# A four-layer graph network on one core: layer 1 writes its inner sums of adj^T to DRAM, layer 3 loads them as operands

## The chip, the cores and the metric

The kernel runs on one core of a Trainium2 chip. The metric is the device time of one execution in microseconds (us), as the median of several runs. Engines are named as in the profile: PE is the matrix engine (PEld its weight loads), DVE the vector engine, ACT the scalar engine, POOL the GpSimd engine and SP the sync engine. SP and POOL issue the DMAs, each in its own queue.

## What is computed

Four graph layers run one after the other on `x` (2708 rows, 512 features) and one sparse-valued, densely stored matrix `adj` (2708 x 2708, fp32). Each layer normalizes its input, aggregates it over the graph and projects it:

```python
h = relu(layernorm(x))
x = x + relu(dinv * ((adj + I) @ (dinv * h)) @ w0)          # layer 0
h = relu(layernorm(x))
x = x + ((dis * (adj @ (dis * h))) @ W.T + b)               # layer 1
h = relu(layernorm(x))
x = x + relu(dinv * ((adj + I) @ (dinv * h)) @ w2)          # layer 2
h = relu(layernorm(x))
# layer 3: gates from adj @ h, masked softmax of scores over adj
x = x + sigmoid(attn_a * (attn @ (h @ W_sa))
                + attn_b * (adj @ (h @ W_gcnb) + b_gcnb))   # layer 3
```

Layers 0 and 2 use `adj` with a diagonal of ones added, layers 1 and 3 use it plain. All four aggregate over the same matrix.

## The kernel before, in words

**Tiling.** The 2708 nodes are cut into four quarters of 677. Of each quarter 640 rows are five tiles of 128 (`KT` is 5); the 37 left over go into two tail tiles. `adj^T` lies in DRAM as blocks `yb[j, i, u]`: quarter `j` of the rows, quarter `i` of the columns, half `u` of those columns. One block is 128 partitions x 5 x 339 fp32, 847.5 KB. `h` stays on chip, and `agg` holds the transposed result of the aggregation.

**Two levels of a fast product.** `aggregate` (line 665) computes `h^T adj^T` with a seven-product scheme in place of eight, at two levels. The outer level splits `h` into XA, XB, XC, XD and `adj^T` into a 2 x 2 of big blocks; `OUTER` (line 426) lists the seven outer products 1 to 7, each with its left operand and the name of its right one. The right operand is a part of `adj^T` (`y11`, `y21`, `y22`) or a sum of such parts (`t1` to `t4`), which layer 0 has computed and kept in DRAM as `osum`. The order of a layer is 1, 7, 2, 4, then the tails of two quarters, 6, 5, then the tails of the other two, then the projection of the first half of the tiles (`epilogue(H1)`), then 3, then `epilogue(H2)`.

Each outer product (`outer_product`, line 516) runs twice, for u = 0 and u = 1. Call one such run a stage. A stage loads the four blocks o11, o12, o21, o22 of its right operand (`load_o`, line 438, issued from SP). Then `inner_y` (line 500) adds on DVE the inner sums of the same scheme: t1 = o12 + o11 (line 509), t2 = o22 + t1 (line 510), t4 = o21 + t2 (line 511), and t3 = o22 + o12, written over o12 (line 513). If the right operand carries a diagonal that has to go, or lacks one, `add_loops` (line 454) first corrects o11 and o22. The operands are numbered 1 (o11), 2 (o21), 3 (o22), 4 (t4), 5 (t1), 6 (t2), 7 (t3). `multiply` (line 544) runs the seven inner products in the order 1, 6, 2, 7, 5, 4, 3, each over five row tiles (`product`, line 535), and puts their sums together on DVE and ACT.

**Buffers.** Blocks live in seven places of `obuf`; the list `free` hands them out in turn, and a stage gives its four back at its end. The sums t1, t2, t4 take slots of `tpool`, which has three under one tag. A slot or a place is used again when all that reads it is done.

**Order of the work.** The program is written in order of layers; the framework's scheduler then sets one fixed order of instructions for every engine and queue, with waits between them, and instructions on one engine need not keep the order of the text. In layer 3 other work lies between the products: dot products of `h` with score vectors (`h_dots`, line 997), row scales (line 1074), and reloads of `h` (`again`, line 1062). Layers 1 and 3 both call `aggregate` with `self_loops` false (lines 961 and 1188), so their inner sums are the same numbers. After layer 3's aggregation follows the attention part, from line 1189 on, which doesn't use the inner sums.

**On POOL's queue** in layer 1 are the loads of `x` tiles (`load_x`, line 911) and the stores of the new ones (line 932), both in `next_x`.

Of the kernel before, what the change touches and what calls it, by code (L numbers as in the profile page):

```python
# [8 lines left out]
FP = mybir.dt.float32  # L9
# [3 lines left out]
P = 128  # L13
# [5 lines left out]
KT = Q // P  # L19
R0 = 32  # L20
R1 = Q - KT * P - R0
U = 2
W = (Q + 1) // U
# [14 lines left out]
def gnn_kernel(  # L38
# [20 lines left out]
    nc = tc.nc  # L59
# [3 lines left out]
    tpool = ctx.enter_context(tc.tile_pool(name="tpool", bufs=3))  # L63
# [4 lines left out]
    dram = ctx.enter_context(tc.tile_pool(name="dram", bufs=1, space=bass.MemoryType.DRAM))  # L68
# [12 lines left out]
    for k in range(1, P // G):  # L81
# [10 lines left out]
    dinv = const.tile([P, NT], FP, name="dinv")  # L92
    dis = const.tile([P, NT], FP, name="dis")
# [7 lines left out]
    xs = [dram.tile([P, D], FP, name=f"xs{t}") for t in range(NT)]  # L101
# [5 lines left out]
        for a in range(2)  # L107
        for b in range(2)
        for u in range(U)
    }  # L110

    h = big.tile([P, NT, D], FP, name="h")
# [14 lines left out]
    free = list(in_obuf)  # L127
# [285 lines left out]
    def other_roots():  # L413
# [12 lines left out]
    OUTER = {  # L426
        1: (XA, "y11", 1),
        2: (XC, "y21", 0),
        3: (XC, "y22", 1),
        4: (XD, "t4", 2),  # L430
        5: (XB, "t1", 1),
        6: (XA, "t2", 2),
        7: (XA, "t3", 1),
    }
    PLAIN = {"y11": (0, 0), "y12": (0, 2), "y21": (2, 0), "y22": (2, 2)}
    QUAD = [(0, 0), (0, 1), (1, 0), (1, 1)]

    def load_o(key, a, b, u):
        blk = free.pop(0)
        if key in PLAIN:  # L440
            j, i = PLAIN[key]
            nc.sync.dma_start(blk, yb[j + a, i + b, u])
        else:
            nc.sync.dma_start(blk, osum[key, a, b, u])
        return blk
# [8 lines left out]
    def add_loops(blk, u, times):  # L454

        for k in range(KT):
            lo, hi = max(k * P, u * W), min((k + 1) * P, (u + 1) * W)
            if lo < hi:
                o = blk[:, k, lo - u * W : hi - u * W]
                nc.vector.scalar_tensor_tensor(  # L460
                    o, ident[:, lo - k * P : hi - k * P], float(times), o, ALU.mult, ALU.add
                )

    def by_halves(f, *xs):

        for ts in (slice(0, KT), slice(KT, 2 * KT)):
            f(*(x[:, ts] for x in xs))

    def minus_sum(o, a, b):
        nc.vector.scalar_tensor_tensor(o, a, -1.0, b, ALU.mult, ALU.subtract)  # L470
# [12 lines left out]
    def inner_x(X, s3=None):  # L483
        n = half // 2
        x11, x12 = X[:, 0:n, 0:P], X[:, n : 2 * n, 0:P]
        x21, x22 = X[:, 0:n, P : 2 * P], X[:, n : 2 * n, P : 2 * P]
        s1, s2, s4 = (
            spool.tile([P, U * W], FP, tag=f"s{k}", name=f"s{k}")[:, 0 : KT * P].rearrange(
                "p (k f) -> p k f", k=KT
            )  # L490
            for k in (1, 2, 4)
        )
        if s3 is None:
            s3 = inner_x3(X)
        minus_sum(s2, x22, s3)
        nc.vector.tensor_sub(s1, x21, x22)
        nc.vector.tensor_add(s4, x12, s2)
        return {1: x11, 2: x12, 3: s4, 4: x22, 5: s1, 6: s2, 7: s3}

    def inner_y(blks, u, loops, t3=None, t3_first=False):  # L500
        o11, o12, o21, o22 = blks
        if loops:
            add_loops(o11, u, loops)
            add_loops(o22, u, loops)
        t1, t2, t4 = (tpool.tile([P, KT, W], FP, tag="t", name=f"t{k}") for k in (1, 2, 4))
        t3 = o12 if t3 is None else t3
        if t3_first:
            nc.vector.tensor_add(t3, o22, o12)
        nc.vector.tensor_add(t1, o12, o11)
        nc.vector.tensor_add(t2, o22, t1)  # L510
        at_y.append(nc.vector.tensor_add(t4, o21, t2).ins)  # L511
        if not t3_first:
            at_y[-1] = nc.vector.tensor_add(t3, o22, o12).ins
        return {1: o11, 2: o21, 3: o22, 4: t4, 5: t1, 6: t2, 7: t3}

    def outer_product(p, self_loops, *dests, at=None):

        X, key, times = OUTER[p]
        with tc.issue_after(at) if at is not None else nullcontext():
            xs_ = inner_x(X)  # L520
        if key in PLAIN:
            loops = times if self_loops else 0
        else:
            loops = 0 if self_loops else -times
        for u in range(U):
            blks = [load_o(key, a, b, u) for a, b in QUAD]
            with tc.issue_after(at) if at is not None else nullcontext():
                ys = inner_y(blks, u, loops)
            multiply(xs_, ys, u, dests)
            free.extend(blks)  # L530

# [100 lines left out]
    def tails(self_loops, qs, loaded=None):  # L632


        at = at_pe[-1]
        for n, q in enumerate(qs):
            blk, pieces = loaded[n] if loaded else tail_rows(self_loops, q)
            for u in range(U):
                tl = pieces[u]
                ps = [  # L640
                    (ps_agg if c < NC - 1 else ps_out).tile(
                        [P, W], FP, tag="agg" if c < NC - 1 else "out", name="pt"
                    )
                    for c in range(NC)
                ]
                with tc.issue_after(at) if loaded else nullcontext():
                    tail_products(ps, tl, True)
                for c in range(NC):
                    d = agg[:, c // 2, q // 2, c % 2, q % 2, u * W : (u + 1) * W]
                    at_end.append(nc.vector.tensor_add(d, d, ps[c]).ins)  # L650
            if blk is not None:
                free.append(blk)
# [5 lines left out]
    def first_part_of_both():  # L658
        nc.scalar.copy(agg[:, 0, 1], agg[:, 0, 0])
# [2 lines left out]
        nc.vector.tensor_add(agg[:, 1, 1], agg[:, 1, 1], agg[:, 0, 1])  # L662
        nc.vector.tensor_add(agg[:, 1, 0], agg[:, 1, 0], agg[:, 1, 1])

    def aggregate(self_loops, epilogue, hooks=None):


        def outer(p, *dests):
            outer_product(p, self_loops, *dests)
            if hooks is not None and p in hooks:  # L670
                hooks[p]()

        outer(1, (0, 0, "as it is"))
        first_part_of_both()
        by_halves(nc.vector.tensor_sub, XA, XA, XB)
        outer(7, (1, 1, "as it is"))
        nc.vector.tensor_sub(XB, XB, XD)
        outer(2, (0, 0, "added"))
        minus_sum(XA, XD, XA)
        nc.vector.tensor_add(XC, XC, XA)  # L680
        outer(4, (1, 0, "as it is"))
        tails(self_loops, (0, 1))
        outer(6, (0, 1, "added"))
        ends_of_sums()
        outer(5, (0, 1, "less"), (1, 1, "less"))
        tails(self_loops, (2, 3))
        epilogue(H1)
        outer(3, (0, 1, "added"))
        epilogue(H2)
# [221 lines left out]
    def load_x(t, src):  # L911
        xt = take(xt_places)
        nc.gpsimd.dma_start(xt, src[t])
        return xt

    def next_x(ts, w_sb, scale, bias, src, colscale, after=None):
        for g in groups(ts):
            n, t0 = len(g), g[0]
            mv = small.tile([P, KT, 2], FP, tag="mv", name="mv")
            xts = []  # L920
            for s, t in enumerate(g):
                xt = load_x(t, src)
                po = project(w_sb, t)
                y = new_y()
                if bias is None:
                    nc.scalar.activation(y, po, AF.Relu, scale=scale[:, t : t + 1])
                else:
                    nc.vector.scalar_tensor_tensor(
                        y, po, scale[:, t : t + 1], bias, ALU.mult, ALU.add
                    )  # L930
                nc.vector.tensor_add(xt, xt, y)  # L931
                nc.gpsimd.dma_start(xs[t], xt)  # L932
                stats(xt, mv[:, s, :])
                xts.append(xt)
            rstd = rstd_of(mv, n)
            if colscale is not None:
                nc.vector.tensor_mul(rstd[:, :n], rstd[:, :n], colscale[:, t0 : t0 + n])
            sh = shift_of(mv, rstd, n)
            for s, t in enumerate(g):
                normalized(t, xts[s], rstd[:, s : s + 1], sh[:, s : s + 1])  # L940
                if after is not None:
                    after(t)
# [15 lines left out]
    w1_sb = load_w(w1)  # L958
    b1_bc = misc[:, 0:D]
    nc.gpsimd.dma_start(b1_bc, b1.partition_broadcast(P))  # L960
    aggregate(False, lambda ts: next_x(ts, w1_sb, dis, b1_bc, xs, dinv))


    def broadcast_columns(po, cs):
# [105 lines left out]
    hooks = {p: lambda ts=ts: h_dots(ts) for p, ts in parts.items()}  # L1070
# [85 lines left out]
    sums = misc[:, 0 : 2 * U * W + NQ * (R0 + R1)]  # L1156
# [28 lines left out]

    hooks[6] = row_scales
    hooks[3] = lambda: again(range(half, NF), slice(0, D // 2))
    aggregate(False, gated_and_ready, hooks)
    wsa_sb = load_w(wsa)
    todo = []  # L1190
    for n, (q, u, b) in enumerate(steps):
# [35 lines left out]
        elif todo:  # L1227
            t, se_t = todo.pop(0)
# [70 lines left out]
```

## Time and profile before

| what | value |
|---|---|
| median of 3 runs | 2097.07 us (2093.76 to 2097.89) |
| profiled execution | 2098.61 us |
| its span in the profile | 2096.7 us |
| granted PE clock, mean | 0.997 |
| layer 1, from its first product to its last projection | about 452 to 833 us |
| layer 3, aggregation and first part of the gates | about 1215 to 1620 us |
| moved by DMA | 360.86 MB |
| HBM read, written | 294.61 MB, 62.15 MB |

The profile is of one execution. Busy time is summed for each engine; the idle time just before an instruction is given together with what ended it. "DMA share" is the mean busy share of the core's 16 DMA engines. A line such as L510 is a line of the kernel before, as printed above. An instruction in the profile that reads `t<-obuf,t` writes the buffer family `t` and reads `obuf` and `t`. SPq and POOLq are the DMA queues of SP and POOL.

### The profile page before, as it was taken

To read this page: it belongs to the slowest core of one execution; us is meant where nothing else is said; L and a number is where in the kernel's file an instruction comes from. 1 tells how busy PE (TensorE), PEld (TensorE's weight loads), DVE (VectorE), ACT (ScalarE), POOL (GpSimd) and SP (SyncE) were. 2 spreads that over 40 slices of the span, in tenths; PEclk is the share of its full clock that TensorE was granted. 3 is DMA by queue.
4 is the path that set the end of the run, shared out by engine and by line. 5 is a ranking of instruction groups with operands and counts; after the bars stand their busy time and mean duration, and the time that the engine had idled before them with its cause. 6 is when DMAs were issued, how large, how long until landed. Compare 5 with 4: busy or idle time off the path is not lost.

```text
span 2096.7 us, 20100 instructions
## 1 busy us (share of the span) xinstructions
PE 2054.8 (98%) x7340; PEld 1279.6 (61%) x7340; DVE 1416.4 (68%) x2481; ACT 409.2 (20%) x833; POOL 182.8 (9%) x330
## 2 busy tenths in 40 slices
PE   5999999999999999999999999999999999999998
PEld 2566655656666554666665556666777666666665
DVE  4578877657767777766686889867538755666512
ACT  1430001130000011100002120000117533444411
POOL 0110111120000012000002120000001000000011
PEclk9999999999999999999999999999999999999999
DMA  9998594555545354654445574555451223233220
GB/s 368 302 373 260 188 342 171 188 190 170 175 154 186 126 189 136 242 174 161 166 145 175 195 244 164 169 166 183 153 176 59 101 99 117 81 103 102 90 74 26
DMA packets 79746, 360.86 MB, mean 172 GB/s; under 512 B 10668, under 2 KB 15660, under 8 KB 79520
## 3 DMA queue, kind: packets, MB, share of 16 engines
q1 hardware_dynamic: 50672, 245.43, 34.0%
q0 software_dynamic: 28976, 114.15, 16.8%
q8 instruction: 58, 0.95, 0.2%
q14 instruction: 40, 0.33, 0.0%
HBM read 294.61 MB, written 62.15 MB: 170 GB/s over the span
## 4 chain that ended last, share of the span: by engine, by line
PE 87%; DVE 6%; DMA 4%; issue 1%; ACT 1%; POOL 0%; SPq 0%; POOLq 0%; DVEq 0%; ACTq 0%
PE pe L1202 17%; PE po L200 15%; PE pc L538 14%; PE pd L538 14%; PE pa L538 13%; PE pb L538 7%; PE pt L600 3%; DMA obuf<-in_yb_dram 2%; DMA ends<-in_yt_dram 1%; PE pt L605 1%; PE pe L600 1%; DVE ends L1001 1%; DMA ends<-xs 1%; PE dg_ps L321 1%; DVE t L511 0%
## 5 line engine op out<-in xcount | busy, mean ns | idle before, releaser
L1202 PE MATMUL pe<-obuf,h 128*128 128x339 f32 x1280 | 373.2, 448 | 0.0
L200 PE MATMUL po<-ends,agg 128*128 128x512 f32 (+2 forms) x968 | 352.1, 521 | 1.3 <-DVE ends L1058 1.0
L538 PE MATMUL pa<-obuf,h 128*128 128x339 f32 x1040 | 317.1, 449 | 2.5 <-ACT h L252 1.4
L1202 PEld LDWEIGHTS pe<-obuf,h 128*128 128x128 f32 x1280 | 240.8, 189 | 127.1 <-issue 10.8
L200 PEld LDWEIGHTS po<-ends,agg 128*128 128x128 f32 x968 | 181.3, 190 | 154.3 <-issue 137.4
L538 PEld LDWEIGHTS pa<-obuf,h 128*128 128x128 f32 x1040 | 195.6, 190 | 110.0 <-issue 9.8
L1119 ACT ACTIVATE e<-r,nsr 128x339 f32<-128x339 f32 x352 | 170.9, 565 | 25.0 <-DVE obuf L1123 11.5
L538 PE MATMUL pb<-t,s 128*128 128x339 f32 x560 | 171.2, 452 | 1.8 <-DVE s L470 1.0
L538 PE MATMUL pc<-t,h 128*128 128x339 f32 x560 | 169.5, 448 | 2.1 <-DVE u L585 2.1
L538 PE MATMUL pd<-t,s 128*128 128x339 f32 x560 | 169.0, 448 | 0.0
L538 PE MATMUL pd<-obuf,s 128*128 128x339 f32 x550 | 166.5, 448 | 1.3 <-DVE s L554 0.9
L572 ACT COPY v<-pa 128x339 f32<-128x339 f32 x56 | 24.6, 439 | 724.7 <-PE pa L538 698.8
L538 PEld LDWEIGHTS pb<-t,s 128*128 128x128 f32 x560 | 106.2, 190 | 57.2 <-DVE t L510 2.1
L538 PEld LDWEIGHTS pc<-t,h 128*128 128x128 f32 x560 | 105.7, 189 | 57.3 <-DVE u L585 3.6
L538 PEld LDWEIGHTS pd<-t,s 128*128 128x128 f32 x560 | 105.8, 189 | 54.1
L538 PEld LDWEIGHTS pd<-obuf,s 128*128 128x128 f32 x550 | 104.0, 189 | 55.2 <-DVE s L554 1.5
L538 PE MATMUL pc<-obuf,s 128*128 128x339 f32 x450 | 136.0, 448 | 0.0
L538 PEld LDWEIGHTS pc<-obuf,s 128*128 128x128 f32 x450 | 85.1, 189 | 43.8 <-issue 0.5
L510 DVE TENSOR_TENSOR t<-obuf,t 128x1695 f32<-128x1695 f32 x55 | 105.5, 1918 | 0.0
L932 POOL DMA_DIRECT2D xs<-ends x66 | 35.9, 544 | 782.4 <-DVE ends L931 706.8
L1219 DVE COPY agg<-pe 128x339 f32<-128x339 f32 x16 | 7.5, 507 | 137.0 <-PE pe L605 137.0
L578 DVE TENSOR_TENSOR u<-v,pb 128x339 f32<-128x339 f32 x56 | 28.4, 507 | 106.1 <-PE pb L538 106.0
(273 smaller groups left out, 2225.9 us busy)
## 6 DMA issues: line engine op xcount, KB each, us to landing
obuf<-in_yb_dram SPq DMA_DIRECT2D x132, 847.5 KB, 4.6
obuf<-osumt SPq DMA_DIRECT2D x100, 847.5 KB, 4.5
osumt<-obuf POOLq DMA_DIRECT2D x22, 847.5 KB, 12.2
xs<-ends POOLq DMA_DIRECT2D x66, 256.0 KB, 2.3
ends<-xs POOLq DMA_DIRECT2D x61, 256.0 KB, 3.9
obuf<-in_yt_dram SPq DMA_DIRECT2D x28, 339.0 KB, 3.5
obuf<-in_yb_dram POOLq DMA_DIRECT2D x11, 847.5 KB, 10.8
ends<-in_yb_dram SPq DMA_DIRECT2D x9, 847.5 KB, 9.5
```

The lines of the kernel that those rows point to most:

```text
L200: nc.tensor.matmul(po, cs[c], ws[c], start=(c == 0), stop=(c == NC - 1))
L321: nc.tensor.matmul(ps[g], first, y, start=n < 4, stop=n >= len(ops) - 4)
L510: nc.vector.tensor_add(t2, o22, t1)
L538: last = nc.tensor.matmul(ps, x[:, k, :], y[:, k, :], start=start and k == 0, stop=k == KT - 1, skip_group_check=not start,)
L572: at_v.append(nc.scalar.copy(v, pa).ins)
L578: at_u2.append(nc.vector.tensor_add(u2, v, pb).ins)
L600: nc.tensor.matmul(ps[c], h[:, NF, c * P : (c + 1) * P], tl[:, 0, :], start=start, stop=False)
L605: nc.tensor.matmul(ps[c], h[g, NF + 1, c * P : (c + 1) * P], tl[g, 1, :], start=False, stop=True)
L932: nc.gpsimd.dma_start(xs[t], xt)
L1001: nc.vector.tensor_tensor_reduce(y, h[:, t, :], vs[:, k, :], 1.0, 0.0, ALU.mult, ALU.add, hd[:, t, k : k + 1])
L1119: nc.scalar.activation(e[:, k], row, AF.Exp, bias=nsr[:, t, s : s + 1], scale=1.0)
L1202: nc.tensor.matmul(pe[c], h[:, t, c * P : (c + 1) * P], a, start=(t == 0), stop=False)
```

## The change

Layer 1 keeps its inner sums. After the four adds of a stage, four DMAs on POOL's queue write t2, t3, t1 and t4 (numbers 6, 7, 5, 4) to DRAM tiles `isum[p, u, k]`: 7 outer products x 2 halves x 4 sums. Layer 3 calls `kept_operands` in place of loading four blocks and adding: it loads the three blocks o11, o21, o22 and the four sums, seven DMAs on SP's queue, in the order in which the products use them. Sum 7 goes into a place of `obuf`, where o12 and t3 had been, and sums 6, 5 and 4 into the slots of `tpool`. Diagonal corrections of blocks 1 and 3 stay; the stored sums already hold them. Layers 0 and 2 are as before.

```diff
--- before.py
+++ after.py
@@ -109,6 +109,13 @@
         for u in range(U)
     }
 
+    isum = {
+        (p, u, k): dram.tile([P, KT, W], FP, name=f"isum{p}{u}{k}")
+        for p in range(1, 8)
+        for u in range(U)
+        for k in (4, 5, 6, 7)
+    }
+
     h = big.tile([P, NT, D], FP, name="h")
 
     agg = big.tile([P, 2, 2, 2, 2, U * W], FP, name="agg")
@@ -513,7 +520,27 @@
             at_y[-1] = nc.vector.tensor_add(t3, o22, o12).ins
         return {1: o11, 2: o21, 3: o22, 4: t4, 5: t1, 6: t2, 7: t3}
 
-    def outer_product(p, self_loops, *dests, at=None):
+    def kept_operands(p, u, loops):
+
+        key, ys, blks = OUTER[p][1], {}, []
+        for k in (1, 6, 2, 7, 5, 4, 3):
+            if k < 4:
+                ys[k] = load_o(key, *{1: (0, 0), 2: (1, 0), 3: (1, 1)}[k], u)
+                blks.append(ys[k])
+                continue
+            if k == 7:
+                ys[k] = free.pop(0)
+                blks.append(ys[k])
+            else:
+                ys[k] = tpool.tile([P, KT, W], FP, tag="t", name=f"t{k}")
+            nc.sync.dma_start(ys[k], isum[p, u, k])
+        if loops:
+            add_loops(ys[1], u, loops)
+            add_loops(ys[3], u, loops)
+        return ys, blks
+
+    def outer_product(p, self_loops, *dests, at=None, sums=None):
+
 
         X, key, times = OUTER[p]
         with tc.issue_after(at) if at is not None else nullcontext():
@@ -523,9 +550,15 @@
         else:
             loops = 0 if self_loops else -times
         for u in range(U):
-            blks = [load_o(key, a, b, u) for a, b in QUAD]
-            with tc.issue_after(at) if at is not None else nullcontext():
-                ys = inner_y(blks, u, loops)
+            if sums == "kept":
+                ys, blks = kept_operands(p, u, loops)
+            else:
+                blks = [load_o(key, a, b, u) for a, b in QUAD]
+                with tc.issue_after(at) if at is not None else nullcontext():
+                    ys = inner_y(blks, u, loops)
+            if sums == "keep":
+                for k in (6, 7, 5, 4):
+                    nc.gpsimd.dma_start(isum[p, u, k], ys[k])
             multiply(xs_, ys, u, dests)
             free.extend(blks)
 
@@ -662,11 +695,11 @@
         nc.vector.tensor_add(agg[:, 1, 1], agg[:, 1, 1], agg[:, 0, 1])
         nc.vector.tensor_add(agg[:, 1, 0], agg[:, 1, 0], agg[:, 1, 1])
 
-    def aggregate(self_loops, epilogue, hooks=None):
+    def aggregate(self_loops, epilogue, hooks=None, sums=None):
 
 
         def outer(p, *dests):
-            outer_product(p, self_loops, *dests)
+            outer_product(p, self_loops, *dests, sums=sums)
             if hooks is not None and p in hooks:
                 hooks[p]()
 
@@ -958,7 +991,7 @@
     w1_sb = load_w(w1)
     b1_bc = misc[:, 0:D]
     nc.gpsimd.dma_start(b1_bc, b1.partition_broadcast(P))
-    aggregate(False, lambda ts: next_x(ts, w1_sb, dis, b1_bc, xs, dinv))
+    aggregate(False, lambda ts: next_x(ts, w1_sb, dis, b1_bc, xs, dinv), sums="keep")
 
 
     def broadcast_columns(po, cs):
@@ -1185,7 +1218,7 @@
 
     hooks[6] = row_scales
     hooks[3] = lambda: again(range(half, NF), slice(0, D // 2))
-    aggregate(False, gated_and_ready, hooks)
+    aggregate(False, gated_and_ready, hooks, "kept")
     wsa_sb = load_w(wsa)
     todo = []
     for n, (q, u, b) in enumerate(steps):
```

## The prediction

> **What bounds the kernel now.** I read the page's engine line, then the groups that the change touches, then the matrix engine's (PE's) own timeline for holes, then busy time and DMA rate in short windows, then who waits on the load queue.
>
> The page: busy time per engine with its share of the span; two of the four groups of adds in question (line, engine, operation, output<-inputs, count | busy us, mean ns | idle before); last, the sizes and times to landing of the DMAs most like the new ones.
>
> ```profile
> PE 2054.8 (98%) x7340; PEld 1279.6 (61%) x7340; DVE 1416.4 (68%) x2481; ACT 409.2 (20%) x833; POOL 182.8 (9%) x330
> ...
> L510 DVE TENSOR_TENSOR t<-obuf,t 128x1695 f32<-128x1695 f32 x55 | 105.5, 1918 | 0.0
> ...
> obuf<-osumt SPq DMA_DIRECT2D x100, 847.5 KB, 4.5
> osumt<-obuf POOLq DMA_DIRECT2D x22, 847.5 KB, 12.2
> ```
>
> PE is busy 98% of the span; the adds are on DVE, at 68%. What DVE is spared counts only where PE waited for it. The timeline of PE in layer 3 (start, length, and in brackets what ended an idle time):
>
> ```profile
> 1223.00 3.70 PE L200 MATMUL po<-ends 128*128 128x512 f32 x8 [1.66 <-DVE ends L178]
> ...
> 1267.79 3.12 PE L538 MATMUL pb<-t,s 128*128 128x339 f32 x10 [0.97 <-DVE s L470]
> ...
> 1305.05 3.02 PE L538 MATMUL pa<-obuf,h 128*128 128x339 f32 x10
> 1307.91 3.02 PE L538 MATMUL pb<-t,s 128*128 128x339 f32 x10
> ...
> 1325.05 3.02 PE L538 MATMUL pa<-obuf,h 128*128 128x339 f32 x10
> ...
> 1484.03 0.84 PE L600 MATMUL pt<-obuf,h 128*128 128x339 f32 x2 [0.57 <-DVE agg L650]
> ```
>
> Products start every 2.86 us (1305.05 to 1307.91), and a stage, the seven products of one half u, takes 20.0 us (1305.05 to 1325.05, gap-free). Laying each start against the end of the group before, I find 8.6 us of holes from 1180 to 1626: 1.82 at 1223, 1.13 at 1267.8, 0.73 at 1484, 0.86 and 0.32 at 1581, 1.18 at 1594, the rest steps of about 0.1 where the matmul's form changes.
>
> Busy us of PE, its weight loads, DVE, ACT and POOL in windows, then granted clock, DMA share and GB/s. First three windows of layer 0 with reads and writes in flight, then a stage of layer 1, then two of layer 3:
>
> ```profile
> 140.00:150.00 10.00, 10.00 (x36) 6.63 (x36) 9.64 (x11) 2.70 (x6) 0.00 (x0) 1.00 1.02 421
> 180.00:190.00 10.00, 10.00 (x36) 6.63 (x36) 10.00 (x13) 0.44 (x1) 0.00 (x0) 1.00 1.02 373
> 240.00:242.00 2.00, 2.00 (x8) 1.32 (x7) 2.00 (x3) 0.00 (x0) 0.42 (x1) 1.00 0.95 380
> 493.00:513.00 20.00, 20.00 (x72) 13.25 (x71) 16.65 (x17) 3.23 (x3) 0.00 (x0) 1.00 0.52 174
> 1234.00:1254.00 20.00, 20.00 (x71) 13.24 (x70) 18.78 (x52) 2.87 (x5) 4.96 (x8) 1.00 0.80 279
> 1294.00:1314.00 20.00, 20.00 (x72) 13.25 (x71) 20.00 (x35) 0.70 (x2) 0.00 (x0) 1.00 0.52 174
> ```
>
> A stage moves 174 GB/s today. PE is full even where DVE is full (1294 to 1314), and where the DMA engines were full in layer 0. The load queue's waits from 370 to 720:
>
> ```profile
> SPq L444 <- PE pd L538: 65.9, 8, 8.7
> SPq L444 <- PE pa L538: 56.2, 15, 5.3
> ```
>
> Loads wait for PE to release blocks, not PE for loads: the transfers have slack.
>
> **What the Trainium skill says.** "Trainium Kernel Development and Optimization", Performance Expectations, warns that matmul busy time is a bad measure because matmuls are pipelined. The trace agrees: a group is 3.02 us long but the next starts after 2.86, so I count holes and starts, not busy time. "VectorE: DVE Perf Modes", the section on the TRN2 errata, gives an fp32 two-input add (N+151)/0.96 ns: 1923 for N = 1695; measured 1918. "SBUF — State Buffer", Who interferes with whom, says that a `tensor_tensor` does not starve the descriptor writing of DMAs issued from GpSimd. The trace agrees: four such writes between 170 and 178 took 0.53 to 0.56 us each while DVE was full. "DMA: Bandwidth & Descriptors", Issuing engines are not separate DMA queues, says that all queues share the same 16 DMA engines; so new writes and old loads are to be added up. It puts a core's HBM limit at about 358 GB/s; this trace shows 421 over 10 us, so I use the trace.
>
> **The change, part by part.**
>
> Layer 3, adds removed: 7 products x 2 halves x 4 adds = 56, at 1.92 us = 107 us of DVE, or 7.7 us per stage. Of PE's holes, two lie behind such adds: before 1267.8 DVE ran a t4 add (L511, 1264.66, 1.93 us) and then the small L470 that PE waited for; before 1484.0 a t4 add (L511, 1480.79, 1.92 us) and then L650. These 1.13 + 0.73 = 1.9 us go, plus some 0.1 of a late L559 near 1260.8. The hole at 1223 isn't theirs: DVE ran no such add from 1182 to 1223.8, but residual sums, statistics and score dots. Those near 1581 and 1594 follow row sums and scalar-engine chains. **Gain 2.0 us.** What is late next there is PE itself.
>
> Layer 3, loads: 3 blocks + 4 sums instead of 4 blocks: 7 x 0.868 MB (847.5 KB) = 6.07 MB per 20.0 us stage, 304 GB/s instead of 174; under the 373 to 421 shown. SP issues 3 more per stage at 0.32 us, 1 us in 20. The new wait: sums 6, 5, 4 of the next stage need a `tpool` slot, freed by products 6, 5, 4 of this stage, 5.7, 14.3 and 17.2 us after its start (2nd, 5th, 6th of seven). On SP the remaining loads queue behind each. Sum 6 is used 22.9 us after that start, sum 5 at 34.3, sum 4 at 37.2: 17.2 us of cover each. Blocks 2 and 7, behind sum 6, are used at 25.7 and 28.6; block 3, behind sum 4, at 37.2 or later; block 1 of the stage after, issued at about 17.2, has over 20. Landing is 4.5 us in the median, 12.2 under traffic. **Cost 0**, hidden by products; uncovered, every us of landing beyond 17.2 would be a us of PE. The diagonal additions L460 stay on blocks 1 and 3; they are 0.29 us pieces on an emptier DVE: 0.
>
> Layer 1, writes: 56 x 0.868 = 48.6 MB, four per stage. With four loads, 8 x 0.868 = 6.94 MB per 20.0 us: 347 GB/s. The trace bounds the mixed rate: 373 to 421 in the windows above, 380 for writes nearly alone; two 2 us windows at 184 to 188 had 292 and 317. I take 373 or better: 18.6 us per stage, so it fits, and PE ran gap-free beside such traffic. New waits: a `tpool` slot and the block of t3 are free only when the write has landed as well. In the stage from 473.6 the next stage's t1 add ran at 479.9, t3 at 482.4, t2 at 488.4, t4 at 492.6. The writes so start about 14 to 0 us before that next stage's start. At the 12.2 us landing, t2's slot would come free up to 9 us into the stage; the following t1 add, now at 6.2, shifts by 3 at worst, and its t2 must wait for product 5 at 14.3 anyway. The block of t3 is held by product 7 until 11.4, longer than the write. **Cost 0; bounds 0 to +31 us** (292 GB/s, worked as in the first rival). No gain from below: nothing in layer 1 is removed.
>
> POOL queue in layer 1: 56 issues at 0.55 us, 31 us, beside a POOL idle for most of that time (0.00 of 20 in the stage above). Behind a write waiting for an add stand `x` loads and `xs` stores of the epilogues. But adds for the stage after an epilogue end before that epilogue's projections, and the epilogue's results for half H2 are first needed after a whole outer product (40 us). Cost 0 to +1; I take 0.
>
> **Sum:** 2098.6 (profiled execution; span 2096.7 and 1.9 around it) - 2.0 = 2096.6. The median of the runs is 1.5 lower, 2097.1, which gives **2095**.
>
> **Rivals.**
>
> Slower, layer 1 becomes DMA-bound. Decides at 347 GB/s. For: 0.52 share at 174 GB/s would be full at 335 if efficiency didn't rise with traffic; the 292 and 317 windows. Against: it does rise, 1.02 at 421. At their mean, 305, a stage needs 22.8 us, 2.8 too many: 22 over the eight stages before the first tails, less some 7 us of cover (the last block's 11.9 us from release to its add, less 4.5 landing), is 15; four more stages give 11 - 7 = 4. 2095 + 19 = **2114**. (At 292: 3.8 per stage, 30 - 7 and 15 - 7 make the 31 above.)
>
> Slower, layer 3's loads late where traffic is dense: around 1234 to 1254 the DMA share is 0.80 already, with weight loads and stores. The longest landing of an `osum` transfer was 24.4 us, 7.2 beyond cover; for the two crowded stages +14: **2109**. Against: only layer 0 showed that.
>
> Faster than forecast: instructions on an engine aren't in program order (t3's add, last in the text, runs before t2's), so without the adds the order is made anew, and the holes at 1223, 1581 and 1594 (4.2 us) may close too: **2091**. Against: none waited for an add.
>
> That the change fails to cut DVE work can't be: loads replace the adds one for one.
>
> **Chances.** 0.2% is 4.2 us, about what a measurement of this kernel can tell from no change. Forecast 0.55, own range 2093 to 2099; DMA-bound layer 1 0.19; late loads 0.06; faster 0.20. So faster 0.20 (below 2092.9), same 0.55, slower 0.25 (above 2101.3). Range 2090 to 2110: it takes in the forecast, the faster case and the late loads, and leaves out nearly all of the DMA-bound case.
>
> **What would show it.** Right: DVE about 107 us less busy; windows of layer 1 near 347 GB/s and of layer 3 near 304, PE still at 20.00 of 20; the holes at 1267.8 and 1484.0 gone. Wrong: PE holes released by DMAs or by adds waiting for a slot in layer 1; stages longer than 20.0; DMA share at 1 in layer 1 with less than 347 GB/s; a different PE order between layers 2 and 3.

## The result, and the profile after

The change makes the kernel slower: 2118.86 us (median of 4 runs, 2115.32 to 2124.64) against 2096.27 (4 runs), a ratio of 1.0111 with an interval of [1.0086, 1.0137]. The forecast was 2095 us with a range up to 2110; the measured time is 8.9 us above the end of that range. The profiled execution took 2124.64, the slowest of the four, with a span of 2122.9; it shows the places well, and some 6 us more than the median.

Below, line numbers are those of the changed kernel where its profile is shown: products are L571 (L538 before), diagonal corrections L467 (L460 before), the copy of a product's sum into `v` is L605 (L572 before), the attention tile's activation L1171 (L1138 before).

The page of the changed kernel: busy time by engine, the group of diagonal corrections, and the sizes and landing times of the new DMAs that carry t2, t1 and t4.

```profile
PE 2061.0 (97%) x7340; PEld 1283.2 (60%) x7340; DVE 1318.9 (62%) x2425; ACT 409.1 (19%) x833; POOL 212.7 (10%) x386
...
L467 DVE SCALAR_TENSOR_TENSOR obuf<-ident,obuf 128x128 f32<-128x128 f32 (+1 forms) x168 | 36.3, 264 | 78.6 <-DMA obuf<-osumt 44.9
...
isum<-t POOLq DMA_DIRECT2D x42, 847.5 KB, 7.5
t<-isum SPq DMA_DIRECT2D x42, 847.5 KB, 4.4
```

DVE is 97.5 us less busy (107 were forecast), and the new transfers land quickly in the median: 7.5 us for writes, 4.4 for loads. Yet 36 us of diagonal corrections have 78.6 us of waiting ahead of them, 44.9 of it for blocks of `osum`; in the kernel before it was 38.2 us, 11.2 of it for these blocks. The waits of PE (engine, line waited for; total us, times, longest) name two that in the kernel before came to 1.1 and 1.0 us in all:

```profile
PE pa L571 <- ACT v L605: 11.5, 3, 10.5
PE pb L571 <- DVE s L477: 5.7, 1, 5.7
```

**Where the time went.** I compared the start of the second product of every stage in the two profiles. "At the third stage" below means between the second product of the second stage and that of the third. The offset is +1.05 us before layer 1, grows by 11.4 over layer 1 (8.5 of it between its second and its fourth stage), falls by 2.0 between layer 1 and the second stage of layer 3, jumps by 12.3 at the third stage of layer 3, and changes by -0.8 from there to the end of PE's work. The span ends 7.7 us after the end of the last instruction, 3.5 before: +4.2. Together these are 26.1 us; the spans differ by 26.2.

**First stall, layer 1.** The timeline of the changed kernel (start, length, idle time before and what ended it):

```profile
497.77 0.61 DVE L467 SCALAR_TENSOR_TENSOR obuf<-ident,obuf 128x45 f32<-128x45 f32 x3 [6.45 <-DMA obuf<-osumt]
498.29 0.50 DVE L592 TENSOR_TENSOR agg<-pc,u 128x339 f32<-128x339 f32 x1
498.71 1.48 DVE L474 TENSOR_TENSOR h<-h 128x1280 f32<-128x1280 f32 x1
500.11 1.92 DVE L518 TENSOR_TENSOR t<-obuf,t 128x1695 f32<-128x1695 f32 x1
...
502.37 0.81 DVE L477 SCALAR_TENSOR_TENSOR s<-h,s 128x640 f32<-128x640 f32 x1
...
503.24 5.66 PE L571 MATMUL pb<-t,s 128*128 128x339 f32 x10 [5.73 <-DVE s L477]
```

DVE stands for 6.45 us before L467, a correction of block o11 for the fourth stage, which PE needs only a stage later. L477, which PE needs at once for the second product of the third stage, stands behind it in DVE's order, and so do L592, L474 and L518. The load of that block started at 486.1, when product 7 of the second stage gave its place free, and landed after 11.6 us. Its counterpart in the kernel before started at 485.1 and landed after 4.5. The shortest, median and longest landing of these loads between 470 and 510 us, in the kernel before and in the changed one:

```profile
DMA to landing us min/median/max: 4.3/4.5/4.5
DMA to landing us min/median/max: 6.0/6.8/11.6
```

PE loses 5.7 us idle and 2.6 more because the product after the hole takes 5.66 us in place of 3.02.

**Second stall, layer 3.** The same view in the second stage (POOL lines are issues of DMAs):

```profile
1256.72 3.02 PE L571 MATMUL pb<-t,s 128*128 128x339 f32 x10
...
1260.53 0.75 POOL L1070 DMA_DIRECT2D ends<-in_wab_dram  x1 [8.68 <-DMA ends<-in_wg_dram]
...
1262.90 0.54 POOL L946 DMA_DIRECT2D ends<-xs  x1
...
1269.20 0.63 ACT L1171 ACTIVATE ends<-ends 128x512 f32<-128x512 f32 x1 [16.37 <-DMA ends<-xs]
1269.74 0.42 ACT L605 COPY v<-pa 128x339 f32<-128x339 f32 x1
1270.21 6.02 PE L571 MATMUL pa<-obuf,h 128*128 128x339 f32 x10 [10.47 <-ACT v L605]
```

PE waits 10.47 us for a copy of 0.42 us, which stands on ACT behind L1171; that one waits for a tile of `x`, whose load stands on POOL behind two gate weights, and the first of these lands late. In the kernel before, ACT had the two in the other order, and the longest wait of POOL for those weights in this stretch was 4.1 us:

```profile
490.19 0.61 DVE L460 SCALAR_TENSOR_TENSOR obuf<-ident,obuf 128x45 f32<-128x45 f32 x3
...
1246.33 3.02 PE L538 MATMUL pb<-t,s 128*128 128x339 f32 x10
1246.53 0.44 ACT L572 COPY v<-pa 128x339 f32<-128x339 f32 x1 [2.31 <-PE pa L538]
...
1249.42 0.54 POOL L913 DMA_DIRECT2D ends<-xs  x1
...
1255.65 0.63 ACT L1138 ACTIVATE ends<-ends 128x512 f32<-128x512 f32 x1 [8.68 <-DMA ends<-xs]
```

The L460 line is the counterpart of the late L467: same place on DVE, no wait. So ACT's order is new, DVE's isn't.

The order weighs more than the lateness. Counted from the second product of the stage (1246.33 and 1256.72), the tile of `x` was asked for 3.1 us after it in the kernel before and 6.2 us after it in the changed one, and L1138 and L1171 began 9.3 and 12.5 us after it. The tile is thus some 3 us later, of a hole of 10.5. In the kernel before ACT waited 8.68 us for it at no cost to PE, since the copy to `v` had gone ahead. The same holds in every run below: where the copy goes first PE has no such hole, though in e8_tiny the activation began 11.1 us after that product; where the activation goes first (e2_loads, e4_diag) the hole is 9.6 and 10.4 us. Why the scheduler set the order of ACT so is not shown.

**The rates.** Windows of the changed kernel (busy PE, PEld, DVE, ACT, POOL; then clock, DMA share, GB/s), the start of layer 1, one of its later stages and one of layer 3; below it the first window in the kernel before:

```profile
453.00:473.00 20.00, 20.00 (x72) 12.80 (x68) 11.49 (x20) 4.58 (x8) 5.08 (x9) 1.00 0.94 323
473.00:493.00 20.00, 20.00 (x71) 13.24 (x70) 13.04 (x17) 0.88 (x2) 2.13 (x4) 1.00 0.98 368
553.00:573.00 20.00, 20.00 (x71) 13.24 (x70) 12.38 (x18) 0.44 (x1) 2.13 (x4) 1.00 0.95 347
1330.00:1350.00 20.00, 20.00 (x72) 13.23 (x71) 5.24 (x12) 0.44 (x1) 0.00 (x0) 1.00 0.91 304
```

```profile
453.00:473.00 20.00, 20.00 (x71) 13.06 (x70) 11.97 (x24) 4.35 (x8) 3.30 (x6) 1.00 0.78 272
```

The later stages move 347 and 304 GB/s, as worked out in the prediction, and PE is full in them. But in the first 20 us of layer 1 the kernel before moved 272 already: beside 2.60 MB of blocks on SP's queue, POOL's queue moved 2.83 MB, tiles of `x` in and out and a weight, for the epilogue that ends there. With writes at 173, four a stage, the demand is 445 by my estimate, more than the 421 that the prediction's windows had shown. What moved in the first two windows was 323 and 368, at a DMA share of 0.94 and 0.98: together less than the demand of 445 and 347. The 323 is also well under the 373 that the prediction had taken for the rate of mixed traffic. A share near 1 in layer 1 with less than 347 GB/s is a sign of being wrong that it had named. The late block shared the DMA engines with one more load, asked for at 483.3, and with writes asked for at 483.1, 486.8 and 491.6.

### The profile page after: what moved, and what is told of

Same layout as the page of the kernel before. It is cut to its first block, busy times and chain, and to the rows that moved or that the text cites. A ratio compares the mean times of both kernels' runs of the same rounds, so it can differ in the third digit from the quotient of the medians.

```text
span 2122.9 us, 20256 instructions
## 1 busy us (share of the span) xinstructions
PE 2061.0 (97%) x7340; PEld 1283.2 (60%) x7340; DVE 1318.9 (62%) x2425; ACT 409.1 (19%) x833; POOL 212.7 (10%) x386
## 4 chain that ended last, share of the span: by engine, by line
PE 87%; DVE 5%; DMA 5%; issue 2%; ACT 0%; POOL 0%; SPq 0%; POOLq 0%; DVEq 0%; ACTq 0%
PE pe L1235 17%; PE po L207 16%; PE pa L571 14%; PE pc L571 13%; PE pd L571 13%; PE pb L571 7%; PE pt L633 3%; DMA obuf<-in_yb_dram 2%; DMA obuf<-osumt 1%; PE pt L638 1%; PE pe L633 1%; DMA ends<-xs 1%; PE dg_ps L328 1%; DVE t L518 0%; PE pl L1003 0%
## 5 line engine op out<-in xcount | busy, mean ns | idle before, releaser
L571 PE MATMUL pa<-obuf,h 128*128 128x339 f32 x1040 | 321.2, 454 | 12.9 <-ACT v L605 11.5
L571 PEld LDWEIGHTS pa<-obuf,h 128*128 128x128 f32 x1040 | 197.3, 191 | 122.3 <-ACT v L605 13.2
L571 PE MATMUL pb<-t,s 128*128 128x339 f32 x560 | 173.7, 457 | 6.5 <-DVE s L477 5.7
L571 PE MATMUL pc<-t,h 128*128 128x339 f32 x560 | 169.4, 448 | 1.3 <-DVE u L618 1.3
L571 PE MATMUL pd<-t,s 128*128 128x339 f32 x560 | 169.0, 448 | 0.0
L605 ACT COPY v<-pa 128x339 f32<-128x339 f32 x56 | 24.6, 439 | 743.3 <-PE pa L571 720.7
L571 PE MATMUL pd<-obuf,s 128*128 128x339 f32 x550 | 166.4, 448 | 0.8 <-DVE s L587 0.5
L571 PEld LDWEIGHTS pb<-t,s 128*128 128x128 f32 x560 | 107.7, 193 | 63.2 <-DVE s L477 6.3
L571 PEld LDWEIGHTS pc<-t,h 128*128 128x128 f32 x560 | 105.8, 189 | 56.3 <-DVE u L618 2.4
L571 PEld LDWEIGHTS pd<-t,s 128*128 128x128 f32 x560 | 105.9, 189 | 54.1
L571 PEld LDWEIGHTS pd<-obuf,s 128*128 128x128 f32 x550 | 104.0, 189 | 54.6 <-DVE agg L592 1.2
L571 PE MATMUL pc<-obuf,s 128*128 128x339 f32 x450 | 136.1, 448 | 0.0
L571 PEld LDWEIGHTS pc<-obuf,s 128*128 128x128 f32 x450 | 85.4, 190 | 43.8 <-issue 0.5
L467 DVE SCALAR_TENSOR_TENSOR obuf<-ident,obuf 128x128 f32<-128x128 f32 (+1 forms) x168 | 36.3, 264 | 78.6 <-DMA obuf<-osumt 44.9
## 6 DMA issues: line engine op xcount, KB each, us to landing
obuf<-in_yb_dram SPq DMA_DIRECT2D x126, 847.5 KB, 4.7
obuf<-osumt SPq DMA_DIRECT2D x92, 847.5 KB, 4.6
isum<-t POOLq DMA_DIRECT2D x42, 847.5 KB, 7.5
t<-isum SPq DMA_DIRECT2D x42, 847.5 KB, 4.4
osumt<-obuf POOLq DMA_DIRECT2D x22, 847.5 KB, 10.1
isum<-obuf POOLq DMA_DIRECT2D x14, 847.5 KB, 8.9
```

The lines of the kernel that those rows point to most:

```text
L467: nc.vector.scalar_tensor_tensor(o, ident[:, lo - k * P : hi - k * P], float(times), o, ALU.mult, ALU.add)
L571: last = nc.tensor.matmul(ps, x[:, k, :], y[:, k, :], start=start and k == 0, stop=k == KT - 1, skip_group_check=not start,)
L605: at_v.append(nc.scalar.copy(v, pa).ins)
```

## The experiments

All medians are beside runs of the kernel before on the same chip. The columns in the middle come from the profile of each, against that of before: growth over layer 1 (from its first stage to the first of layer 2), the jump at the third stage of layer 3, the end of PE's work, and the time after the last instruction.

| kernel | median - before, us | ratio [interval] | layer 1 | stage 3 of layer 3 | end of PE | after last instruction |
|---|---|---|---|---|---|---|
| before | 0 | | | | | 3.5 |
| changed kernel | +22.6 | 1.0111 [1.0086, 1.0137] | +11.4 | +12.3 | +21.9 | 7.7 |
| e1_writes | +8.3 | 1.0042 [1.0027, 1.0057] | +6.0 | -1.5 | +4.6 | 7.7 |
| e2_loads | +11.4 | 1.0053 [1.0038, 1.0068] | 0.0 | +11.1 | +7.9 | 3.2 |
| e3_act | +12.4 | 1.0063 [1.0047, 1.0078] | +9.1 | +2.9 | +13.7 | 7.7 |
| e4_diag | +16.1 | 1.0077 [1.0060, 1.0093] | +5.2 | +11.8 | +16.3 | 7.7 |
| e5_both | +6.3 | 1.0030 [1.0021, 1.0040] | +5.0 | -1.1 | +0.7 | 7.7 |
| e6_some | +4.3 | 1.0025 [1.0017, 1.0033] | +2.3 | -1.3 | +0.1 | 6.5 |
| e7_before_act | +0.5 | 1.0001 [0.9992, 1.0010] | 0.0 | -0.7 | +2.9 | 3.5 |
| e8_tiny | +4.5 | 1.0019 [1.0013, 1.0026] | +0.3 | +0.3 | +3.4 | 7.7 |
| e10_tiny_twice | +2.0 | 1.0011 [1.0003, 1.0019] | 0.0 | -1.4 | -0.6 | 3.8 |
| e11_tiny_sp | +2.5 | 1.0011 [1.0004, 1.0018] | +5.7 | -0.8 | +4.5 | 3.5 |
| e12_some_sp | +1.3 | 1.0005 [0.9997, 1.0014] | +1.2 | -1.2 | -3.6 | 3.5 |
| e13_tiny_84 | +3.2 | 1.0012 [1.0005, 1.0019] | +0.7 | -1.2 | -0.2 | 6.6 |

Profiles differ by up to 2 us before layer 1 begins (e12_some_sp and e2_loads by -2.0 and -1.9), so the two columns of growth say more than the end of PE. At the third stage of layer 3 the profile of before has its hole of 1.13 us, and kernels that still add there have one of 0 to 1.1, so that -1.1 in that column means no hole and not always a gain of the change.

**The two halves of the change, each alone.** e1_writes has layer 1 write its sums and layer 3 add as before:

```diff
-    aggregate(False, gated_and_ready, hooks, "kept")
+    aggregate(False, gated_and_ready, hooks)
```

> The writes of layer 1 alone; layer 3 loads four blocks and adds, as before. Theory (two waits in in-order queues: in layer 1 a diagonal addition on DVE that waits for a late load, in layer 3 a copy on ACT that waits for a late tile): the PE hole of about 6 us at the third stage of layer 1 and the slow matmuls after it stay (8.5 us in all), some 3 us at the tails of layer 1 too, and layer 3 has no hole above 2 us: 10 to 12 us over the kernel before. Rival (the seven loads per stage in layer 3 are what costs): within 3 us of the kernel before. Rival (DMA traffic slows every stage of layer 1): stages of layer 1 longer than 20.0 us throughout.

e2_loads has no writes; layer 3 loads something of the same size in place of each sum, blocks of adj^T from the input:

```diff
-    aggregate(False, lambda ts: next_x(ts, w1_sb, dis, b1_bc, xs, dinv), sums="keep")
+    aggregate(False, lambda ts: next_x(ts, w1_sb, dis, b1_bc, xs, dinv))
...
-            nc.sync.dma_start(ys[k], isum[p, u, k])
+            nc.sync.dma_start(ys[k], yb[p % 4, k % 4, u])
```

> The loads of layer 3 alone: nothing is written in layer 1, and layer 3 loads its four sums per stage from blocks of the input of the same size, so its aggregate is another one than the reference's. Theory: layer 1 as before, and in the second stage of layer 3 a PE hole of about 10 us behind an ACT copy that waits for an x tile, slow matmuls after it; 10 to 12 us over the kernel before. Rival (all the loss comes from the writes): 2 us under the kernel before.

Measured +8.3 and +11.4 us, of the whole change's 22.6; the rest is some interaction or the scatter of layer 1's stall. Both halves cost time, each in its own layer. In e1_writes the stall of layer 1 is one stage earlier, with the same shape:

```profile
486.33 0.65 DVE L467 SCALAR_TENSOR_TENSOR obuf<-ident,obuf 128x128 f32<-128x128 f32 x3 [2.80 <-DMA obuf<-osumt]
...
488.86 0.50 DVE L618 TENSOR_TENSOR u<-u,pc 128x339 f32<-128x339 f32 x1
...
489.41 3.12 PE L571 MATMUL pc<-t,h 128*128 128x339 f32 x10 [2.32 <-DVE u L618]
```

A late block stops DVE at L467, and L618, for which PE waits, is behind it.

**Is it the order on ACT?** e3_act is the changed kernel with the activations of the attention tiles held back until the last copy to `v` of layer 3's aggregation is issued (the first then runs at 1564 us); e7_before_act is the same edit to the kernel before.

```diff
-        nc.scalar.activation(xt, xt, AF.Copy, bias=0.5)
+        with tc.issue_after(at_v[-1]):
+            nc.scalar.activation(xt, xt, AF.Copy, bias=0.5)
```

> The changed kernel, with the attention part's copies of x tiles on ACT ordered behind the last v copy of the aggregation. Theory: the hole in the second stage of layer 3 is gone and layer 1's stays: 10 to 13 us under the changed kernel, 9 to 12 over the kernel before. Rival (the hole comes from a late sum or block, and ACT's wait is only beside it): a hole of about the same size ended by a DMA, no gain over the changed kernel.

> The kernel before, with only the attention part's copies on ACT behind the last v copy. Theory: this order in itself costs and brings nothing there, since ACT's wait covered no v copy that PE needed: within 2 us of the kernel before. Rival (the new order is worth something by itself): 3 us or more under it.

The jump at the third stage of layer 3 shrinks from 12.3 to 2.9 us, and the distance from the kernel before from 22.6 to 12.4; in the kernel before the edit changes nothing that can be measured. So ACT's order is the larger part of layer 3's stall, and a gain only where the new loads had changed it. What remains at that stage is a new hole:

```profile
1272.36 0.61 DVE L467 SCALAR_TENSOR_TENSOR obuf<-ident,obuf 128x45 f32<-128x45 f32 x3 [2.15 <-DMA obuf<-osumt]
...
1274.26 0.50 DVE L592 TENSOR_TENSOR agg<-pd,u 128x339 f32<-128x339 f32 x1
...
1274.81 4.81 PE L571 MATMUL pd<-obuf,s 128*128 128x339 f32 x10 [2.16 <-DVE agg L592]
```

It is layer 1's pattern: a correction of a late block, L467, and behind it on DVE the sum that PE waits for.

**Is it the order on DVE?** e4_diag holds the diagonal corrections (and, in layer 1, the adds of the same stage with them) back until the sum of the previous stage's second product (line 611) is issued; e5_both has this and e3_act's edit.

```diff
-                    ys = inner_y(blks, u, loops)
+                    with tc.issue_after(at_u2[-1]) if loops else nullcontext():
+                        ys = inner_y(blks, u, loops)
...
-            add_loops(ys[1], u, loops)
-            add_loops(ys[3], u, loops)
+            with tc.issue_after(at_u2[-1]):
+                add_loops(ys[1], u, loops)
+                add_loops(ys[3], u, loops)
```

> The changed kernel, with the diagonal additions of a stage ordered on DVE behind the first u sum of the stage before it. Theory: layer 1's hole at the third stage is gone, layer 3's stays: 7 to 9 us under the changed kernel, 13 to 16 over the kernel before. Rival (layer 1 lacks DMA bandwidth and the load would be late for PE itself): a hole of 4 us or more within the two stages that follow, ended by a DMA or by an add that waited for one.

> The changed kernel with both orders put right: the diagonal additions behind the first u sum of the stage before, and the attention part's copies on ACT behind the last v copy. Theory: the jump of 11 to 12 us at layer 3's second stage is gone, small holes of some 5 us stay in layer 1 where other DVE work waits for late loads; 3 to 7 us over the kernel before. Rival (the two holes only move, since the DMA engines are the limit): 10 us or more over the kernel before.

With DVE's order alone, layer 1 loses 5.2 us in place of 11.4; layer 3 keeps its stall, since ACT's order is still that of the changed kernel. The 11.4 can't be compared alone: with the same code in layer 1, e1_writes lost 6.0 and e3_act 9.1. The firmer comparison is e3_act with e5_both, where DVE's order takes the median from +12.4 to +6.3, and the two intervals don't overlap; by the profiles 4.1 us of this lie in layer 1 and 4.0 in layer 3. With both, layer 3 has no stall (-1.1 at its third stage) and the median is +6.3. In layer 1 some 5 us stay, in small holes (the two largest of e4_diag there are 1.1 and 0.8 us, before a sum on DVE). DVE's waits for blocks at L467 between 440 and 860 us are down from 42.6 us to 15 in e4_diag, but those at the add L520 aren't (7.0 us in e4_diag, 5.8 in the changed kernel): a later place on DVE doesn't bring the blocks sooner. I didn't follow these holes further.

**Bytes, or instructions and waits?** e8_tiny is e1_writes with one piece of 64 KB written of each sum, so that all 56 DMAs and their places on POOL stay and nearly all of the traffic goes. e6_some neither keeps nor loads the sums of outer products 1 and 7, the first four stages of a layer.

```diff
-                    nc.gpsimd.dma_start(isum[p, u, k], ys[k])
+                    nc.gpsimd.dma_start(isum[p, u, k][:, 0, 0:128], ys[k][:, 0, 0:128])
```

```diff
-            outer_product(p, self_loops, *dests, sums=sums)
+            outer_product(p, self_loops, *dests, sums=None if p in (1, 7) else sums)
```

> As the writes alone, but each of the 56 writes moves only 128 columns of the first of five rows, 64 KB in place of 847.5 KB: the same DMAs, orders and waits for the buffers, 7.5% of the bytes; layer 3 adds as before. Theory (traffic makes the loads late): holes of layer 1 gone, within 2 us of the kernel before. Rival (buffers held longer by the writes, or the 56 issues on POOL, are what costs): as the writes alone, 7 to 9 us over.

> The changed kernel, but outer products 1 and 7, the first of every layer, neither write nor load sums: layer 3 adds them as before. Theory: the starts of layers 1 and 3, where loads also refill the blocks after an epilogue, are as before; some 3 us at the tails of layer 1 stay and 1 us is won later in layer 3; 1 to 4 us over the kernel before. Rival (every stage with doubled traffic costs alike): 5/7 of the loss of the changed kernel, about 15 us over the kernel before.

With tiny writes layer 1 grows by 0.3 us: its cost is traffic, not issue. A tiny write also lands sooner (3.7 us in place of 7.5 in the changed kernel), so this run alone doesn't clear slots that are held longer. The waits do: in layer 1 DVE waited for the landing of a write once in e1_writes, 2.5 us, and in the changed kernel no wait ended with one, against 36 and 40 us for late blocks at L467. Without the writes of the first four stages layer 1 grows by 2.3, though ten stages still write at the full rate: most of the cost lies in the first stages, beside the epilogue's own traffic, and not in a rate that the whole layer can't hold. In e6_some the stall of layer 3 is gone too; there ACT has the order of the kernel before.

**The end of the span.** Of e8_tiny's +4.5, as much as 4.2 comes after the last instruction in its profile, 7.7 us in place of 3.5. My first theory was a cost for each DMA that POOL issues (0, 40 and 56 of them gave 3.5, 6.5 and 7.7). e10_tiny_twice writes two pieces of each sum (112 DMAs), e13_tiny_84 the second piece for u = 0 alone (84), and e11_tiny_sp issues the 56 tiny writes from SP. Their edits to e8_tiny, in this order:

```diff
+                    nc.gpsimd.dma_start(isum[p, u, k][:, 0, 128:256], ys[k][:, 0, 128:256])
```

```diff
+                    if u == 0:
+                        nc.gpsimd.dma_start(isum[p, u, k][:, 0, 128:256], ys[k][:, 0, 128:256])
```

```diff
-                    nc.gpsimd.dma_start(isum[p, u, k][:, 0, 0:128], ys[k][:, 0, 0:128])
+                    nc.sync.dma_start(isum[p, u, k][:, 0, 0:128], ys[k][:, 0, 0:128])
```

> Layer 1 writes two pieces of 64 KB of each sum, 112 DMAs on POOL; layer 3 adds as before. Theory (the span gets some 75 ns longer after its last instruction for each DMA that POOL issues): 8.4 us at the end instead of 4.2, so the time between last instruction and end of the span is about 12 us instead of the 3.5 of before and the 7.7 with 56 such DMAs; the median some 4 us above that of one tiny write for each sum, about 2106. Rival (the 4.2 us at the end are a fixed cost, or one of layer 1's schedule): 7.7 us again, about 2102.

> Layer 1 writes one piece of 64 KB of each sum and, for the half u = 0, a second one: 84 DMAs on POOL; layer 3 adds as before. The time from the last instruction to the end of the span was 3.5, 6.5, 7.7 and 3.8 us with 0, 40, 56 and 112 added POOL DMAs. Theory (it grows with the count by 75 ns and starts anew somewhere between 56 and 112): either near 9.8 us, or below 7.7 by a start before 84. Rival (it is an effect of the order that the scheduler set with one write for each sum, not of the count): 3.5 us. Median 2098 to 2105.

> The tiny writes of 64 KB, 56 of them, are issued by SP instead of POOL; layer 3 adds as before. Theory (the end is longer by the DMAs of POOL alone): the time after the last instruction is 3.5 us again. Rival (each DMA that writes to DRAM costs it): 7.7 us. Where the loads now queue behind a write that waits for its add, holes in layer 1 may come: bounds 0 to 6 us. Median 2097 to 2104.

From SP the end is 3.5 us, so it is POOL's DMAs that lengthen it. But 84 of them gave 6.6 and 112 gave 3.8. (In e10_tiny_twice the last instruction, the issue of a store, ends at 2092.6 in a span of 2096.4.) The theory of 75 ns for each falls, and so does the one with a single restart of the count: 84 and 112 don't lie on one such line with 56. The profile does name what runs last. It is a DRAIN of POOL, the longest of three at the kernel's last line (shortest, median and longest in ns; start of the first and of the last), here of the kernel before and of the changed one:

```profile
L1295 POOLq DRAIN x3: 46/102/3012, 2092.6 to 2096.2; - x3
L1328 POOLq DRAIN x3: 46/102/7504, 2114.6 to 2122.6; - x3
```

In the changed kernel the last store has landed 6.3 us before the end of the span, and the DRAIN ends 0.8 us before it. It lasts 3.0 us in all five profiles without added DMAs on POOL, and 6.3, 7.5, 6.4 and 3.5 with 40, 56, 84 and 112 of them, the same 7.5 for writes of 64 KB and of 847.5 KB. So the number of these DMAs matters, and at 56 of them the size doesn't; what sets the length stays open. e11_tiny_sp also shows the price of SP as issuer in layer 1: +5.7 us. On SP the loads stand behind writes that wait for their adds, which is the likely cause; I didn't test it.

**A version to beat both?** e12_some_sp is e6_some with its 40 writes issued by SP.

```diff
-                    nc.gpsimd.dma_start(isum[p, u, k], ys[k])
+                    nc.sync.dma_start(isum[p, u, k], ys[k])
```

> The changed kernel, with outer products 1 and 7 neither kept nor loaded (layer 3 adds for them as before), and the remaining 40 writes issued by SP. With POOL as issuer this gave 2101.6, of it 3.0 after the last instruction. Theory (the end is longer by POOL's DMAs alone, and the holes of layer 3 behind adds are worth 2 us): end 3.5 us again, 2098.5 if SP's order costs nothing in layer 1. Rival (SP is in order, so loads queue behind writes that wait for adds; the cover of the loads is used up): new holes in layer 1, 2102 to 2115.

2098.61 against 2097.30: no slower than can be measured, and no faster. At the tails, where it loads the sums, layer 3 gains 0.8 us. The -1.2 at stage 3 is no gain of the loads: there e12_some_sp still adds, and e1_writes and e10_tiny_twice, which add everywhere, have -1.5 and -1.4. Layer 1 gives 1.2 back, and the rest is within the scatter of the runs (2094.8 to 2103.5). With PE full for 98% of the span there is little more for this change to win.

## Why the prediction was wrong, step by step

**Gain 2.0 us in layer 3: right in kind, somewhat large.** No kernel that loads the sums has a hole behind an add at the tails (near 1484), and none that loads them at the third stage has one there; e6_some and e12_some_sp, which still add at that stage, have 0.2 and 0.3. But those holes vary: the seven kernels that still add everywhere in layer 3 (before, e1, e7, e8, e10, e11, e13) have 0 to 1.1 us at the third stage and 0.6 to 1.7 at the tails, in the mean 0.6 + 1.0 = 1.6. The 1.9 was read off one execution.

**Layer 3, loads at cost 0: this step failed.** Its working was right for what it looked at. A later stage moves 304 GB/s and no product waited for a sum: 17.2 us of cover were enough. (Two times of use in it are one product late: sum 5 is used 31.4 us after the stage's start and sum 4 at 34.3, in place of 34.3 and 37.2; the 17.2 hold with the right ones.) It asked only when PE needs the new loads. It took the order of the other engines as given, and left out what the new traffic does to other loads in those stages and who stands behind them. ACT's new order put the copy for PE behind an activation that waits for a tile of `x`, that tile came some 3 us later, and the third stage lost 12.3 us (e2_loads: 11.1 with the loads alone; e3_act: 2.9 with the order undone). "The diagonal additions L460 stay ... 0" failed likewise: 0.29 us pieces, but each waits for a block on an engine that works in order. My rival of late loads in crowded stages had the place and about the size (+14), but by luck: its mechanism was wrong, since it made PE wait for sums. A new order of instructions I had named only as a source of gain.

That one late transfer holds up what stands behind it fits what the Trainium skill says: "PSUM — Partial Sum Buffer", Engine vs sequencer instructions, states that the queues of the scalar, vector and GpSimd engines are strict FIFO. Here three instructions of 0.50, 1.48 and 1.92 us, whose own inputs were ready, waited behind a 6.45 us wait of L467.

**Layer 1, writes at cost 0: this step failed in its demand, its rate and its cover.** The demand of 347 GB/s holds for later stages, and these took 20.0 us. For the first 20 us the sum should have been 272 + 173 = 445: I took the stage that begins at 493, with 174, as every stage's load. The rate I had taken, 373 or better, was not reached there: 323 moved at a share of 0.94. And the cover was counted to the adds, 7.4 us after a landing of 4.5, where the first reader on DVE is the correction L460. In the kernel before it runs at 490.19, 5.1 us after its load started at 485.1, so the cover was 0.6 us. The landing grew by 7.1, to 11.6, and DVE stood still for the difference, 6.45. The first rival, a DMA-bound layer 1, had the resource but not the place; in e6_some ten stages at that rate cost 2.3 us.

**The queue of POOL at 0 to +1:** right in layer 1 (e8_tiny, +0.3). Not foreseen is the end of the span, +4.2, where POOL's DRAIN takes 7.5 us in place of 3.0; no part of the sum had a place for it.

**The sum with what was measured**, from the profiles: -2.0 between layer 1 and the third stage (not tied to the change by any run here), -0.8 at the tails, +11.4 in layer 1, +12.3 in layer 3, +4.2 at the end and +1.05 before layer 1, which the change doesn't touch, are 26.2 of the two spans' difference. The medians differ by 22.6; what of layer 1's stall is scatter (11.4 here, 6.0 and 9.1 with the same code in e1_writes and e3_act) stays open.

## What to carry to other kernels

For every load that becomes later or that shares its stretch with new traffic, find the first instruction that reads it on its in-order engine, and then what stands behind that instruction; the cover is the time to that reader, not to the product that uses the data. Ask also whether a change of instructions may change the order on engines that it doesn't touch, and what that order can put in front of a copy that PE needs. Take the demand on DMA from the busiest stretch, such as the one in which an epilogue's own loads and stores are in flight, not from a steady stage. And where PE is at 98%, look first at how little there is to win: two holes of 1.6 us together, against two layers of added traffic.

## What the runs showed of the hardware

The product after a long hole runs slowly. After 5.7 us idle one took 5.66 us, after 10.5 us one took 6.02, both in place of 3.02; the window of the second:

```profile
1270.00:1275.00 5.00, 4.79 (x9) 2.96 (x10) 4.81 (x19) 0.16 (x1) 0.00 (x0) 0.50 0.00 0
```

The granted clock is 0.50. "TensorE: Matmul & The Clock Gate", Part 1: The HAM clock gate, of the Trainium skill says that after an idle window of about 3.4 us PE's clock is halved until it has been busy for about as long. The two long holes agree as to the half clock, which lasted 5 to 6 us after PE had set in again, and each cost some 3 us more than its length. But no hole need be 3.4 us long. In e3_act the product after a hole of 2.16 us, shown above, took 4.81 us, and from about 1 us after its start the clock was 0.50:

```profile
1276.00:1279.00 3.00, 3.00 (x6) 1.74 (x6) 3.00 (x7) 0.00 (x0) 0.00 (x0) 0.50 0.30 124
```

In e11_tiny_sp a hole of 2.62 us was followed by a product of 4.81 us too, while in e1_writes the product after a hole of 2.32 us took 3.12. With a loss after 2.16 us and none after 2.32, the length of a hole doesn't decide by itself; what does isn't shown here. Where it happened, such a short hole cost 1.8 us more than its length. The other thing not expected is the end of the span, told above.
